# Layer 0 of a four-layer convolution network: the order of two kinds of expansion rows, and the place of some loads

## The chip, the cores and the metric

The kernel runs on one NeuronCore of one Trainium2 chip. The metric is the device time of one execution in microseconds, all four layers in one launch; lower is better. The time before is the median of three runs.

## The reference, cut to what matters

The input `x` is (4, 64, 256, 256) in float32. Four layers follow each other, each `x = x + layer(group_norm(x))`. Only layer 0 is touched by the change:

```python
x = einsum('bchw,oc->bohw', group_norm(x), w_in)      # 64 -> 384 channels: the "expansion"
# every 8x8 patch: rfft2, times a filter per channel, irfft2
x = conv_general_dilated(x, w_dw, padding=1, feature_group_count=C)   # 3x3, per channel
x1, x2 = split(x, 2, axis=1)
x = einsum('bchw,oc->bohw', gelu(x1) * x2, w_out)     # 192 -> 64 channels: the "projection"
```

The later layers are a 3x3 convolution, a thresholded choice between two 1x1 convolutions, and a product in Fourier space.

## The kernel before, in words

Layer 0 works on patches of 8x8 pixels. A batch item has 32 rows of patches. A **block** `p` covers 11 of them plus one row of halo, so there are three blocks for each item and 12 in all (`blocks`, `p` = 0 to 11); the rows of a block are `t` = 0 to 11. The first block of an item has no row `t = 0` and the last has no row `t = 11`, because the image ends there. The hidden channels are worked in four quarters (`kb` = 0 to 3). So there are 48 rounds `(p, kb)`, and each has two parts:

1. **Expansion** (`expand(p, kb, t)` for each row). TensorE multiplies normalized patches (the stationary operand, from `xn`) by the quarter's weights `win` into two PSUM buffers `psu`, one for each half of the image (`s` = 0, 1). ScalarE then copies half 0, and VectorE half 1, from PSUM into the big SBUF tile `u`. There are two kinds of rows. A **paired** row (`pairs` true) puts two patches into one stationary operand of 128 columns (line 444): 16 products in the program, 32 matmul and 32 weight-load instructions in the profile, and four copies on each engine (line 459). An **unpaired** row has one patch per stationary (line 450): 64 matmul and 64 weight-load instructions, and three copies on each engine (lines 461 to 463).
2. **Convolution** (`convolve(p, kb, g)` for 12 groups `g`). The patch filter and the 3x3 convolution are one product with a prepared matrix `w` (lines 494 and 503), then a gelu on ScalarE (line 510), a product on VectorE (line 511) and a store of `g` to DRAM by GpSimd's queue (line 514). Before the groups 0, 3, 6 and 9 stands one `unit()`: a piece of the projection of the block before (`project`, lines 591 and 598, TensorE; lines 607 to 618, VectorE), followed by `load_half`, which asks SyncE for the residual rows (`load_r`, line 559) and the stored `g` (`load_g`, lines 546 and 550) of a later unit.

PSUM is handed out by `banks()`: four buffers of two banks in turn. A row of the expansion takes two, so two rows are in flight; a convolution group takes two, a unit one.

The order on TensorE, VectorE, ScalarE and SyncE is the order of the program (`manual_schedule`). The engines meet by semaphores alone, so SyncE issues each DMA as soon as those before it in its own order are issued and its buffer is free, whatever row TensorE is at. SyncE's loads in a round are: `load_w` (the matrices `w` of a later pair of groups, line 471), `load_half` (in `kb` 0 also at rows 5 and 8), and `load_next`. The last is called four times in a round. For `kb` 0 to 2 it loads a piece of the next item for its group statistics (`load_stats`, line 627), which VectorE works at groups 1, 2, 4 and 5 (`next_stats`, line 320). For `kb` 3 it loads one of the first four new rows of the next block (`load_x`, line 418), which ScalarE normalizes at groups 1, 2, 3 and 4 (line 256).

Of the kernel before, what the change touches and what calls it, by code (L numbers as in the profile page):

```python
# [121 lines left out]
class _Net:  # L122
# [152 lines left out]
    def _layer0(self, ctx, dst):  # L275
# [5 lines left out]
        def banks(name):  # L281

            return pp.tile([128, 2, 512], F32, tag=f"p{next(turn) % 4}", name=name)
# [11 lines left out]
        NR = 11  # L295
# [118 lines left out]
        def load_x(row, p_x=p_x):  # L414
            b, i = row
            x0[row] = p_x.tile([128, P, HW2], F32, tag="x", name=f"x0_{b}_{i}")
            for s in range(2):
                nc.sync.dma_start(x0[row][halves[s]], a["x"][b, :, P * i : P * i + P, s * HW2 : (s + 1) * HW2])

        def normalize_x(row):  # L420
            b, i = row
            xn = xns[row] = p_xn.tile([128, HW2 // P, P, P], F32, tag="xn", name=f"xn_{b}_{i}")
            self.normalize(
                xn.rearrange("p m r w -> p r m w"), x0.pop(row).rearrange("p r (m w) -> p r m w", w=P), 0, b
            )
# [6 lines left out]
        def expand(p, kb, t):  # L432

            b, i0 = blocks[p]
            ps = [banks(f"psu_{p}_{kb}_{t}_{s}") for s in range(2)]
            xn = xns[b, i0 + t]
            lo, hi = halves
            pairs = t % 2 == 0
            for k in range(2):
                for m in range(4):  # L440
                    n, at = 2 * (4 * k + m), slice(2 * PB * m, 2 * PB * (m + 1))
                    for s in range(2):
                        if pairs:
                            nc.tensor.matmul(  # L444
                                ps[s][:, k, at], xn[halves[s], n : n + 2].rearrange("p n r w -> p (n r w)"),
                                win[halves[s], kb, 0 : 2 * PB], start=True, stop=True,
                            )
                            continue
                        for odd in range(2):
                            nc.tensor.matmul(  # L450
                                ps[s][halves[1 - odd], k, at], xn[halves[s], n + odd].rearrange("p r w -> p (r w)"),
                                win[halves[s], kb, PB * (1 - odd) : PB * (3 - odd)], start=True, stop=True,
                            )
            at = lambda h, o: u[h, :, t * CW + o : t * CW + o + 8].rearrange("p c (s m) -> p c s m", s=2)
            for s, copy in enumerate((nc.scalar.copy, nc.vector.tensor_copy)):
                v = ps[s][:, :, 0 : 8 * PB].rearrange("p s (m c) -> p c s m", m=4)
                if pairs:
                    for h, o, k, c in ((lo, O1, lo, 0), (hi, O2, lo, PB), (lo, E1 + 1, hi, 0), (hi, E2 + 1, hi, PB)):
                        copy(at(h, 8 * s + o), v[k, c : c + PB])  # L459
                    continue  # L460
                copy(at(slice(0, 128), 8 * s + 1), v[:, 0:PB])
                copy(at(hi, 8 * s + E2 + 1), v[lo, PB:])
                copy(at(lo, 8 * s + O1), v[hi, PB:])  # L463

        def load_w(j):

            p, k = divmod(j, HID // 8)
            if p >= NB:
                return
            w = wl[j] = p_w.tile([128, 2, 4, NC], F32, tag="w", name=f"w_{j}")  # L470
            nc.sync.dma_start(
                w, wts[k // 8][:, :, :, 4 * (k % 8) : 4 * (k % 8) + 4].rearrange("h i k c n -> (h i) k c n")
            )
# [89 lines left out]
        def load_half(p, r, half):  # L563
            if 0 <= p < NB and r < P:
                if half == 0:
                    load_r(p, r)
                load_g(p, r, half)
# [56 lines left out]
        def load_stats(b, j):  # L624
            t = st[b, j] = p_x.tile([128, 4, W], F32, tag="x", name=f"st{b}_{j}")
            for s in range(2):
                nc.sync.dma_start(t[halves[s]], src_t[b, :, j, s])

        def next_stats(b, j):
            if b not in bst0s:  # L630
                bst0s[b] = new_bst0(b)
            input_stats(st.pop((b, j)), j, bst0s[b])
            if j == NJ - 1:
                self.norms.append(self.group_norm_parts(0, b, bst0s.pop(b)))
# [6 lines left out]
        with ordered:  # L641
# [51 lines left out]
            for p in range(NB + 1):  # L693
                units = iter([(r, half) for r in range(P) for half in range(2)] if p > 0 else [])
                ahead, first = 1, []
                if p == NB:
                    ctx_u.close()
                    sources.append([pool("l0g1e", 6), pool("l0g6e", 6), pool("l0re", 3)])
                    ahead = 3
                for r in range(ahead):  # L700
                    for half in range(2):
                        first.append((p - 1, r, half))
                        if p == NB:
                            load_half(*first.pop())

                def unit():
                    at = next(units, None)
                    if at:
                        project(p - 1, *at)
                        load_half(p - 1, at[0] + ahead, at[1])  # L710

                if p == NB:
                    for k in range(2 * P):
                        unit()
                    while self.norms:
                        self.next_norms()
                    break
                b, i0 = blocks[p]
                rows = rows_of(p)
                after = rows_of(p + 1) if p + 1 < NB else []  # L720
                fresh = [row for row in after if row not in xns]
                for t in (0, NR):
                    if not 0 <= i0 + t < NP:
                        nc.gpsimd.memset(rows_u[:, :, t], 0.0)
                nk = [] if b + 1 >= B else list(range(p % NI * NJ // NI, (p % NI + 1) * NJ // NI))
                loaded, begun = [], iter(fresh[:4])

                def load_next(kb):
                    if kb == 3:
                        row = next(begun, None)  # L730
                        if row:
                            load_x(row)
                    elif nk:
                        loaded.append(nk.pop(0))
                        load_stats(b + 1, loaded[-1])

                for kb in range(4):
                    for t in range(NR + 1):
                        if 0 <= i0 + t < NP:
                            expand(p, kb, t)  # L740
                        if t in (5, 8) and first:
                            load_half(*first.pop(0))
                        if t == NR - 2:
                            load_w(p * (HID // 8) + NG * kb // 2 + 3)
                        if t >= NR - 1:
                            load_next(kb)
                    for g in range(NG):
                        G = NG * kb + g
                        if g % 2 == 0 and g > 0:
                            load_w(p * (HID // 8) + G // 2 + 3)  # L750
                        if g % 3 == 0:
                            unit()
                        convolve(p, kb, g)
                        if g < 2:
                            load_next(kb)
                        if g < NG - 1:
                            self.next_norms()
                        if kb < 3:
                            if g in (1, 2, 4, 5) and loaded:
                                next_stats(b + 1, loaded.pop(0))  # L760
                        elif 0 <= g - 1 < len(fresh):
                            k = g - 1
                            normalize_x(fresh[k])
                            if k + 4 < len(fresh):
                                load_x(fresh[k + 4])
                for row in rows:
                    if row not in after:
                        xns.pop(row)
# [728 lines left out]
```

## Time and profile before

| | us |
|---|---|
| median of 3 runs | 6502.17 |
| lowest, highest run | 6493.61, 6522.05 |
| the profiled execution | 6525.09 |
| its span, first to last instruction | 6523.3 |
| TensorE busy in the span | 6001.2 (92%) |
| VectorE busy | 4272.8 (66%) |
| ScalarE busy | 3240.4 (50%) |

The profiled execution lies 23 us above the median. In lines of the timeline the first number is the start in us from the span's start, the second the length in us, then follow engine, source line, operation, the tile written and the tiles read, and the number of instructions (x32); a bracket gives the idle time before and what ended it. PE is TensorE, PEld its weight loads, DVE is VectorE, ACT is ScalarE, POOL is GpSimd, SPq is SyncE's queue. Layer 0 fills the span up to about 3840 us.

### The profile page before, as it was taken

The numbers are of one execution on the slowest core, as the hardware profiler recorded it, in microseconds if no ns is written. First come the engines' busy times: TensorE is split into PE (matmuls) and PEld (weight loads), VectorE is DVE, ScalarE is ACT, GpSimd is POOL, SyncE is SP. The second block draws the span as 40 slices with busy tenths as digits, with TensorE's granted clock in tenths as the row PEclk, the third lists the DMA queues.
The fourth block names the chain that finished last, engine by engine and source line by source line (L and its number), as shares of the span: only waits on it lengthen the run. The fifth ranks groups of instructions, "written<-read, shape, count | busy, mean of one in ns | idle before, by whom it ended". The sixth has DMA issues, their size and how long they took to land.

```text
span 6523.3 us, 238228 instructions
## 1 busy us (share of the span) xinstructions
PE 6001.2 (92%) x106712; PEld 3199.7 (49%) x106712; DVE 4272.8 (66%) x5924; ACT 3240.4 (50%) x4564; POOL 1046.6 (16%) x1646
## 2 busy tenths in 40 slices
PE   2999999999999999999999977999899999999988
PEld 1455555555555555555555543333344444443566
DVE  5556665565655565655555546999798889885355
ACT  4344434344443444443444314777787778773211
POOL 3111111111111111111111111111122222221011
PEclk9999999999999999999999978999999999999855
DMA  8487879787888787886868779999576666667899
GB/s 242 136 218 214 230 207 232 218 242 219 245 220 243 219 236 206 229 223 199 228 195 226 207 198 244 226 229 228 148 180 174 170 173 181 170 176 268 325 353 398
DMA packets 878510, 1447.67 MB, mean 222 GB/s; under 512 B 77252, under 2 KB 586452, under 8 KB 875444
## 3 DMA queue, kind: packets, MB, share of 16 engines
q1 hardware_dynamic: 725284, 923.09, 55.9%
q0 software_dynamic: 148672, 500.14, 22.1%
q8 instruction: 843, 13.81, 0.9%
q10 hardware_dynamic: 3536, 9.20, 0.6%
q14 instruction: 175, 1.43, 0.1%
HBM read 932.08 MB, written 500.04 MB: 220 GB/s over the span
## 4 chain that ended last, share of the span: by engine, by line
PE 83%; DMA 7%; ACT 5%; issue 2%; DVE 2%; SPq 1%; POOL 0%; ACTq 0%; DVEq 0%; POOLq 0%
PE pc L503 18%; PE pc L494 12%; PE m L880 10%; PE psu L444 9%; PE one L1121 9%; PE div L1080 7%; ACT u L459 4%; PE psu L450 4%; PE po L591 4%; PE psz L1110 2%; DMA x<-x 2%; PE po L598 2%; DMA g<-g 2%; PE psa L1308 2%; DMA x<-in_x_dram 1%
## 5 line engine op out<-in xcount | busy, mean ns | idle before, releaser
L511 DVE TENSOR_TENSOR h<-h,pc 128x374 f32<-128x374 f32 x1152 | 575.3, 541 | 1216.7 <-ACT h L510 1216.5
L510 ACT ACTIVATE h<-pc 128x374 f32<-128x374 f32 x1152 | 493.1, 480 | 1762.0 <-PE pc L503 1745.9
L503 PE MATMUL pc<-u,w 64*16 64x374 f32 (+2 forms) x27648 | 1241.4, 480 | 3.0 <-issue 3.0
L514 POOL DMA_DIRECT2D g<-h x576 | 414.8, 720 | 2990.7 <-DVE h L511 2800.8
L494 PE MATMUL pc<-u,w 64*64 64x374 f32 x9216 | 881.2, 488 | 6.7 <-DVE u L463 3.9
L503 PEld LDWEIGHTS pc<-u,w 64*16 64x16 f32 (+2 forms) x27648 | 413.3, 92 | 763.5 <-issue 761.6
L444 PE MATMUL psu<-win,xn 64*128 64x96 f32 x8704 | 625.7, 283 | 137.2 <-ACT u L459 124.1
L459 DVE COPY u<-psu 64x384 f32<-64x384 f32 x1088 | 604.3, 555 | 155.1 <-PE psu L444 143.5
L444 PEld LDWEIGHTS psu<-win,xn 64*128 64x128 f32 x8704 | 574.8, 193 | 206.2 <-ACT u L459 159.9
L459 ACT COPY u<-psu 64x384 f32<-64x384 f32 x1088 | 560.5, 515 | 221.1 <-PE psu L444 201.0
L1066 DVE TENSOR_TENSOR q<-xn 128x2313 f32<-128x2313 f32 (+2 forms) x256 | 628.0, 2496 | 1.9 <-ACT xn L256 1.7
L1121 PE MATMUL one<-z,wp 32*32 32x512 f32 x16384 | 598.0, 599 | 19.0 <-issue 14.9
L256 ACT ACTIVATE xn<-x,nb,r 128x1024 f32<-128x1024 f32 (+3 forms) x272 | 486.7, 1792 | 212.4 <-DMA x<-x 140.5
L494 PEld LDWEIGHTS pc<-u,w 64*64 64x64 f32 x9216 | 332.2, 132 | 451.1 <-issue 359.7
L1067 ACT ACTIVATE q<-q 128x2313 f32<-128x2313 f32 (+2 forms) x256 | 529.0, 2087 | 30.8 <-DVE q L1066 29.3
L450 PE MATMUL psu<-win,xn 64*64 64x96 f32 x17408 | 456.5, 253 | 79.3 <-issue 48.6
L1080 PE MATMUL div<-q,ones 64*32 64x512 f32 x8192 | 471.1, 602 | 13.8 <-ACT q L1067 10.9
L1121 PEld LDWEIGHTS one<-z,wp 32*32 32x32 f32 x16384 | 367.2, 103 | 229.7 <-issue 88.3
L450 PEld LDWEIGHTS psu<-win,xn 64*64 64x64 f32 x17408 | 396.8, 138 | 121.4 <-issue 66.7
L1154 POOL DMA_DIRECT2D x<-r x512 | 273.9, 544 | 977.8 <-DVE r L1151 963.9
L591 PE MATMUL po<-g,wo 128*64 128x176 f32 (+1 forms) x3072 | 314.9, 348 | 74.3 <-DMA g<-g 37.9
L880 PE MATMUL m<-t,wk 64*64 64x512 f32 x3072 | 341.1, 588 | 0.0
(162 smaller groups left out, 6672.9 us busy)
## 6 DMA issues: line engine op xcount, KB each, us to landing
g<-h POOLq DMA_DIRECT2D x576, 374.0 KB, 6.4
x<-x SPq DMA_DIRECT2D x240, 640.0 KB, 6.4
w<-wt SPq DMA_DIRECT2D x288, 448.0 KB, 7.0
x<-x SPq DMA_DIRECT2D x100, 1024.0 KB, 14.2
g<-g SPq DMA_DIRECT2D x414, 187.0 KB, 5.0
g<-g SPq DMA_DIRECT2D x736, 93.5 KB, 5.3
x<-in_x_dram SPq DMA_DIRECT2D x256, 256.0 KB, 8.2
x<-o POOLq DMA_DIRECT2D x128, 512.0 KB, 8.2
```

Source lines behind the costliest of these rows:

```text
L444: nc.tensor.matmul(ps[s][:, k, at], xn[halves[s], n : n + 2].rearrange("p n r w -> p (n r w)"), win[halves[s], kb, 0 : 2 * PB], start=True ...
L450: nc.tensor.matmul(ps[s][halves[1 - odd], k, at], xn[halves[s], n + odd].rearrange("p r w -> p (r w)"), win[halves[s], kb, PB * (1 - odd) ...
L459: copy(at(h, 8 * s + o), v[k, c : c + PB])
L494: nc.tensor.matmul(out(C * c, C, k, h), w[halves[h], k, 2 * (G % 2) + c, 0:C], cells(h, 4 * g + 2 * k + c, 0, 0), start=True, stop=False, ...
L503: nc.tensor.matmul(out(q, m, k, h), w[halves[h], k, 2 * (G % 2) + c, c0 : c0 + m], cells(h, 4 * g + 2 * k + c, down, right), start=False, ...
L511: nc.vector.tensor_mul(h[:, k], h[:, k], ps[k][:, 1, 0:L])
L591: nc.tensor.matmul(out(k, s, x), wo1, moving(g1[:, 2 * k], 2 * half + k, s, x), start=(x == 0), stop=False, skip_group_check=True,)
L880: nc.tensor.matmul(rows2(m)[halves[j], s], w[dx][halves[s]], ts[n][halves[s], i, 2 * j : 2 * j + 2, dx : dx + W], start=(dx == 0), stop=(d ...
L1066: nc.vector.tensor_sub(d, p0, p1)
L1067: nc.scalar.activation(d, d, AF.Square)
L1080: ins = nc.tensor.matmul(ps[quarters[j], h], ones[halves[h]], q[n, g, k][halves[h], r + 2 * j : r + 2 * j + 2, o : o + W], start=(m == 0), ...
L1121: ins = nc.tensor.matmul(rows2(ps[g])[quarters[j], k], w[quarters[i]], z[quarters[i], h, 2 * j + dy : 2 * j + dy + 2, dx : dx + W], tile_p ...
```

## The change

In `expand`, a row is paired when `t` is below 6, where before it was paired when `t` is even. The numbers of paired and unpaired rows stay the same in every block: 6 and 6, or 5 and 6 in the first block of an item, 6 and 5 in the last. The rows 0 to 5 are now paired and the rows 6 to 11 unpaired.

In the loop over rounds, `load_w` moves from row 9 to row 11 (`NR` is 11), and the four `load_next` calls move from rows 10 and 11 and groups 0 and 1 to row 11 and groups 0, 1 and 2.

```diff
-            pairs = t % 2 == 0
+            pairs = t < (NR + 1) // 2
...
-                        if t == NR - 2:
+                        if t == NR:
                             load_w(p * (HID // 8) + NG * kb // 2 + 3)
-                        if t >= NR - 1:
                             load_next(kb)
                     for g in range(NG):
                         G = NG * kb + g
...
                         convolve(p, kb, g)
-                        if g < 2:
+                        if g < 3:
                             load_next(kb)
```

## The prediction

> **What bounds the kernel now.** I read the costliest groups by shape first, then the timeline of one expansion engine by engine, then the same expansion in time windows, then a stall.
>
> ```profile
> L444 PE MATMUL psu<-win,xn 64*128 64x96 f32 x8704 | 625.7, 283 | 137.2 <-ACT u L459 124.1 <-issue 7.1 <-DVE h L511 5.8
> L450 PE MATMUL psu<-win,xn 64*64 64x96 f32 x17408 | 456.5, 253 | 79.3 <-issue 48.6 <-ACT u L463 24.7 <-ACT xn L256 5.8
> L459 DVE COPY u<-psu 64x384 f32<-64x384 f32 x1088 | 604.3, 555 | 155.1 <-PE psu L444 143.5
> ```
>
> In the 48 expansions TensorE is idle for 137.2 + 79.3 = 216 us. Two causes matter: 124.1 us of waiting for the copies of line 459 (ended by "ACT u L459"), and 55.7 us (48.6 + 7.1) "issue". The convolution has nearly none, so the expansion is where the change can act.
>
> ```profile
> 1503.76 2.20 PE L444 MATMUL psu<-win,xn 64*128 64x96 f32 x32 [0.79 <-ACT u L459]
> 1505.89 1.55 PE L450 MATMUL psu<-win,xn 64*64 64x96 f32 x64
> 1508.06 2.34 PE L444 MATMUL psu<-win,xn 64*128 64x96 f32 x32 [0.62 <-ACT u L459]
> ...
> 1525.82 1.49 PE L591 MATMUL po<-g,wo 128*64 128x160 f32 x16 [0.62 <-ACT u L459]
> ...
> 1576.63 2.03 PE L444 MATMUL psu<-win,xn 64*128 64x96 f32 x32
> ...
> 1505.99 2.26 DVE L459 COPY u<-psu 64x384 f32<-64x384 f32 x4 [0.45 <-PE psu L444]
> 1508.29 0.56 DVE L461 COPY u<-psu 128x384 f32<-128x384 f32 x1
> 1508.86 0.55 DVE L462 COPY u<-psu 64x384 f32<-64x384 f32 x1
> 1509.43 0.56 DVE L463 COPY u<-psu 64x384 f32<-64x384 f32 x1
> 1510.44 2.26 DVE L459 COPY u<-psu 64x384 f32<-64x384 f32 x4 [0.45 <-PE psu L444]
> ```
>
> Two rows take 4.45 us (1505.99 to 1510.44). Neither engine fills that: VectorE copies 2.30 + 1.70 us and idles 0.45, TensorE works 2.03 + 1.55. The cause is that alternate rows give every paired row the same two of the four PSUM buffers. Matmuls (2.03) and VectorE's copies (2.26) of paired rows cannot overlap each other, and with about 0.15 of handing over that loop is 4.45. The unpaired rows' loop (1.55 + 1.70) has slack.
>
> ```profile
> 1503.00:1507.00 4.00, 3.24 (x84) 3.15 (x88) 3.47 (x7) 3.30 (x8) 0.00 (x0) 1.00 1.03 308
> 1507.00:1511.00 4.00, 3.32 (x73) 2.91 (x66) 3.45 (x7) 3.19 (x7) 0.00 (x0) 1.00 1.10 217
> 1515.00:1519.00 4.00, 3.39 (x95) 3.17 (x88) 3.77 (x7) 3.34 (x7) 0.00 (x0) 1.00 0.01 4
> 1361.00:1371.00 10.00, 7.33 (x177) 6.67 (x177) 8.66 (x16) 7.82 (x16) 0.00 (x0) 1.00 1.01 244
> ```
>
> The last three columns are TensorE's clock, DMA share and GB/s. An expansion of kb 1 to 3 (these rows: p 4, kb 2, first row at 1499.45) has full DMA engines for some 11 us, then almost none. In kb 0 (last row: p 4, first row at 1343.13) they are full to the end.
>
> ```profile
> 2204.80 0.54 PE L450 MATMUL psu<-win,xn 64*64 64x96 f32 x11
> 2208.72 2.51 PE L450 MATMUL psu<-win,xn 64*64 64x96 f32 x53 [3.38 <-issue]
> 2211.16 3.73 PE L444 MATMUL psu<-win,xn 64*128 64x96 f32 x32
> q8 instruction: 843, 13.81, 0.9%
> ```
>
> The "issue" idle time is instruction supply. Queue 8 moved 13.81 MB in 843 packets, 16.4 KB each, against 213,424 matmuls and weight loads and some 2,450 semaphore instructions of TensorE: 256 instructions a packet. In the records of the trace the stalls sit at one position in every 256, 1.2 to 1.7 us after the end of a packet, and that packet was asked for one block (256 instructions) earlier. So a block can't be entered sooner than the packet's start delay + 1.14 (median packet) + 1.42 after the block before it; I use delay + 2.55 us.
>
> **The change part by part: the rows.** Now neighbours of one kind use the two buffer pairs in turn, so matmuls of one row run beside copies of the one before. The loops halve: (2.03 + 2.26 + 0.15) / 2 = 2.22 us paired, (1.55 + 1.70 + 0.15) / 2 = 1.70 unpaired. VectorE's own work is longer, 2.30 and 1.73 with its gaps, and becomes the bound; ScalarE copies 2.13 and 1.54 and stays under it. From the first matmul: VectorE starts at 2.11 (1576.63 to 1578.74), works six paired rows to 15.9, and has finished row 9 at 22.8; TensorE then does row 11 in 1.6 and is at the projection at 24.4. Before, that took 26.37 (1499.45 to 1525.82): 1.95 saved. Where row 11 is missing: 22.7 against 24.19, 1.5 saved; where row 0 is missing: 22.1 against 23.56, 1.45. Sixteen expansions of each: 31 + 24 + 23 = **78 us**, of 216 idle. VectorE's last copy ends at 26.3, about when the projection's 2.1 us end, and only the later products of the first group read that row.
>
> **The change part by part: instruction supply.** 256 instructions last 5.9 us in alternation (192 in 4.45), 9.2 in paired rows, but only 3.45 in unpaired ones. The unpaired rows now run from about 14 to 24 us and enter some three blocks. Packet start delays before, medians over the blocks p 1 to 11, by time after the first row: kb 1 and 2: 3.8 us at 4 to 8 us, 1.3 at 12 to 16, 0.9 at 16 to 20, 0.8 at 20 to 24. kb 3: 4.1, 1.5, 2.3, 0. kb 0: 2.1, 2.1, 4.6, 3.6. With 2.55 added, the early ones exceed 5.9 now and won't exceed 9.2; the late ones come near 3.45 in kb 1 to 3 and exceed it twofold in kb 0. I worked each of these 44 expansions through row by row with its own recorded delays. Stalls before, kb 0 to 3: 1.5, 0.9, 0.5, 0.8 us each; after: 4.3, 0.8, 0.6, 1.4. Eleven of each: +31, -1, +1, +6, and some 2 for p 0: **39 us lost**, four fifths of it in kb 0. Bounds: no stalls after at all saves the 40 us of before (3.7 x 11); the late delays of kb 0 in every expansion would add 3.5 x 33 = 115.
>
> A stall also costs clock. Behind the 3.38 us stall above, a paired row takes 3.73 us for 2.03, and the window 2212 to 2216 has a granted clock of 0.50. The records show 15 such drops in layer 0 after p 0, mostly in kb 1 to 3 and after stalls from 1.5 us on; 3.4 to 10 us at half. I expect about as many, moved to kb 0: nothing, within 20 us either way.
>
> [...]
>
> **The change part by part: the loads.** SyncE runs ahead, so the row at which a call stands matters only through its order: at 1499.66, in the first row, it already issues the `load_w` that stands at row 9. `load_w` passes nothing but its own `load_next`: nothing. The second load now stands behind the `load_half` of group 0, whose `load_g` waits for that unit's matmuls; the third and fourth move by a group, the fourth behind `load_w` of group 2. So 512 KB leaves the busy start of the expansion (about 2 us of DMA at 230 to 300 GB/s), which helps supply in kb 0 a little. The second load then goes out where the third does now, at 1532.91, and needs about 7 us (the page: 8.2 for these loads); VectorE wants it at 1540.02. In the records loads from this place land 9 to 12 us after the first convolution matmul and are wanted at 12. If one is 2 us late, VectorE's statistics, and behind them the projection's additions, move; the product of group 3 has 0.39 us and its PSUM buffers about 2 us of cover. ScalarE's normalization in kb 3 is alike. I take 0; a whole microsecond in 38 expansions would be 38.
>
> **Sum.** -78 + 39 = -39 us. Against the profiled execution 6525.1 to 6486; it was 23 us above the median, so against the median 6502 to **6463**.
>
> **Rivals.** (1) Supply keeps up once DMA is idle: in kb 1 to 3 no stall is left. For it: windows with a DMA share of 0.01. Against: delays of 0.8 to 1.5 us are recorded there. -78 + 31 - 24 = -71, 6431; hidden in kb 0 too, -118, 6384. Chance 0.18. [...] (2) No measurable difference: kb 0 pays the clock on top (about two 3.4 us windows at half, some 2 us, in 11 expansions) or loads come late; -39 + 22 = -17, 6485. Against: the second load no longer burdens kb 0. Chance 0.26. (3) Slower: supply of the dense rows. If every late packet of kb 1 to 3 has kb 3's delay of 2.3 us, a block takes 4.85 for 3.45, and 2.5 blocks cost 3.5 us where I count 0.9: 2.6 x 33 = +86, so +47, 6549. It decides from 1.2 us more stall per expansion (39 / 33). For it: no block anywhere in layer 0 took under 4.08 us, so 3.45 is unproven. Against: quiet DMA at that time. Chance 0.13. That the change does nothing is no rival: the paired rows' loop is broken by construction.
>
> **How the numbers follow.** My forecast has 0.43 and its own range 6445 to 6480. Measurement here tells about 0.5% from nothing, 32.5 us, so faster means under 6469.7. The forecast gives 0.34 of that and rival 1 all of its 0.18, with 0.05 from milder forms of rival 2: 0.57. Slower is rival 3, 0.13. The rest, 0.30, is the same. The range 6405 to 6520 leaves out the hidden fetch in full and most of rival 3.
>
> **What would show it.** Right: in paired rows VectorE's copies back to back at 2.3 us; the wait of line 444 for "ACT u L459" down from 124 us to below 40; clean expansions of kb 1 and 2 at 24.4 us for 12 rows; stalls of line 450 under "issue" up from 48.6, mostly in kb 0. Wrong: two paired rows still apart by more than 2.4 us; issue waits of 3 us in unpaired rows of kb 1 and 2; statistics of line 320 waiting for loads at group 2.

## The result, and the profile after

The change takes 6486.01 us (median of 20 runs, 6469.98 to 6506.94) against 6509.86 us for the kernel before in the same session: a ratio of 0.9963, with a 95% interval of 0.9949 to 0.9978. On another chip, with 6 runs, it was 0.9949 (0.9933 to 0.9964). So it is faster by 24 to 33 us where 39 were forecast. By the bound of 0.5% named in the prediction its first measurement counts as "the same", which had a chance of 0.30; "faster" had 0.57. The time lies in the range of 6405 to 6520, but above the forecast's own 6445 to 6480. Times and ratios in this document leave out one slow execution, 10213.84 us at a granted clock of 0.727, of the kernel with kb 0 alternating and kb 3's loads as before.

The two profiled spans, 6523.3 and 6490.0 us, differ by 33.3 us. Layer 0, from its first expansion to its last convolution, holds 22.8 of that; the rest lies in stages that the change does not touch.

The groups by shape after, in the same view as before:

```profile
L444 PE MATMUL psu<-win,xn 64*128 64x96 f32 x8704 | 604.4, 285 | 63.2 <-ACT u L459 40.7 <-DVE h L511 10.9 <-ACT xn L256 7.6
L450 PE MATMUL psu<-win,xn 64*64 64x96 f32 x17408 | 494.0, 252 | 99.8 <-issue 65.7 <-ACT u L459 11.7 <-DVE u L463 8.5
L256 ACT ACTIVATE xn<-x,nb,r 128x1024 f32<-128x1024 f32 x128 | 158.9, 1241 | 149.1 <-DMA x<-in_x_dram 149.0
```

The wait of line 444 for ScalarE's copies fell from 124.1 to 40.7 us; the issue wait before line 450 rose from 48.6 to 65.7. Two things are new. Line 450 is busy 37 us longer than before (456.5), while line 444 is busy 21 us less (625.7 before); a single matmul of line 450 is no longer than before (252 ns, before 253), and the kernel with the rows alone changed shows the same 494 us. And ScalarE's normalization waits 149.0 us for x loads, where it was 68.0.

The timeline of a clean expansion after (p 4, kb 2; TensorE's rows, then VectorE's):

```profile
1481.68 3.81 PE L444 MATMUL psu<-win,xn 64*128 64x96 f32 x64
1485.97 9.10 PE L444 MATMUL psu<-win,xn 64*128 64x96 f32 x128 [0.48 <-ACT u L459]
...
1506.05 1.48 PE L591 MATMUL po<-g,wo 128*64 128x160 f32 x16
...
1483.78 13.75 DVE L459 COPY u<-psu 64x384 f32<-64x384 f32 x24 [0.47 <-PE psu L444]
```

VectorE makes the 24 copies of six paired rows without a pause: 13.75 / 6 = 2.29 us a row. The projection starts 24.37 us after the first row (1481.68 to 1506.05). And the same stretch of kb 0 after (p 4), timeline of TensorE and of one normalization of ScalarE's:

```profile
1319.44 2.20 PE L444 MATMUL psu<-win,xn 64*128 64x96 f32 x32
1322.77 3.39 PE L444 MATMUL psu<-win,xn 64*128 64x96 f32 x32 [1.13 <-DVE h L511]
...
1351.78 2.19 PE L450 MATMUL psu<-win,xn 64*64 64x96 f32 x47 [3.58 <-issue]
1353.90 1.86 PE L591 MATMUL po<-g,wo 128*64 128x160 f32 x16
...
1320.53 1.24 ACT L256 ACTIVATE xn<-x,nb,r 128x1024 f32<-128x1024 f32 x1 [4.34 <-DMA x<-in_x_dram]
```

and one window of it, with the busy time of each engine (TensorE's matmuls first) and at the end the granted clock (TensorE's, 1.00 is full speed), the DMA share and GB/s:

```profile
1325.00:1331.00 6.00, 5.36 (x49) 5.11 (x49) 2.93 (x6) 4.11 (x9) 0.00 (x0) 0.50 0.99 214
```

It lasts 34.5 us against 28.4 before. At its start ScalarE has waited 4.34 us for an x load, in a normalization of the round before, and what stands behind it is late. TensorE then waits 1.13 us for a buffer that VectorE's product of line 511 has to give free, and the window 1325 to 1331 has a granted clock of 0.50. At its end TensorE is idle for 3.58 us under "issue", at the entry of a block of 256 instructions.

By kind of round, from the first row to the projection, means over the blocks p 1 to 11: kb 0 27.2 us before, 31.8 after; kb 1 26.3 and 23.9; kb 2 25.7 and 23.5; kb 3 26.6 and 24.1. So kb 1 to 3 gained 78.5 us in all and kb 0 lost 50.5, with 6.3 more in its first projection piece. The convolution of kb 3 behind that piece got longer by 1.1 us (11 in all).

### The profile page after: what moved, and what is told of

Same layout as the page of the kernel before. It is cut to its first block, busy times and chain, and to the rows that moved or that the text cites. A ratio compares the mean times of both kernels' runs of the same rounds, so it can differ in the third digit from the quotient of the medians.

```text
span 6490.0 us, 238212 instructions
## 1 busy us (share of the span) xinstructions
PE 6025.7 (93%) x106712; PEld 3225.2 (50%) x106712; DVE 4272.2 (66%) x5924; ACT 3239.9 (50%) x4564; POOL 1047.5 (16%) x1646
## 3 DMA queue, kind: packets, MB, share of 16 engines
q1 hardware_dynamic: 725284, 923.09, 56.1%
## 4 chain that ended last, share of the span: by engine, by line
PE 76%; DMA 9%; DVE 7%; ACT 3%; issue 3%; SPq 1%; POOL 0%; DVEq 0%; ACTq 0%; POOLq 0%
PE pc L503 17%; PE pc L494 11%; PE m L879 10%; PE one L1120 9%; PE div L1079 7%; PE psu L444 5%; DVE u L459 5%; PE psu L450 4%; PE po L591 4%; DMA x<-in_x_dram 3%; PE psz L1109 2%; DMA x<-x 2%; DMA g<-g 2%; PE po L598 2%; PE psa L1307 2%
## 5 line engine op out<-in xcount | busy, mean ns | idle before, releaser
L444 PE MATMUL psu<-win,xn 64*128 64x96 f32 x8704 | 604.4, 285 | 63.2 <-ACT u L459 40.7
L256 ACT ACTIVATE xn<-x,nb,r 128x1024 f32<-128x1024 f32 (+3 forms) x272 | 486.8, 1793 | 293.5 <-DMA x<-in_x_dram 149.0
L450 PE MATMUL psu<-win,xn 64*64 64x96 f32 x17408 | 494.0, 252 | 99.8 <-issue 65.7
L450 PEld LDWEIGHTS psu<-win,xn 64*64 64x64 f32 x17408 | 428.4, 136 | 159.4 <-issue 89.9
```

The costliest lines, as they stand in the source:

```text
L444: nc.tensor.matmul(ps[s][:, k, at], xn[halves[s], n : n + 2].rearrange("p n r w -> p (n r w)"), win[halves[s], kb, 0 : 2 * PB], start=True ...
L450: nc.tensor.matmul(ps[s][halves[1 - odd], k, at], xn[halves[s], n + odd].rearrange("p r w -> p (r w)"), win[halves[s], kb, PB * (1 - odd) ...
```

## The experiments

Theory A: what the rows gain is partly given back by the moved x loads of kb 3, which land late and hold ScalarE, in kb 3 and into the next kb 0. Theory B: kb 0 loses because dense rows (the unpaired ones, 128 instructions in some 1.7 us) run there while DMA is full (a share of 1.13 from 1344.54 to 1348.91 us of the kb 0 above) and TensorE's instructions come late. The rivals are named in each expectation. "Rows-only" is the first kernel below.

**Rows grouped, loads as before.** The first hunk of the change alone.

> Rows 0 to 5 paired, 6 to 11 unpaired as in the change; every load where it was before. Theory A (the moved loads cost time: the four loads of kb 3 arrive late, ScalarE waits for them in the normalizations of kb 3 and into the first rows of the next kb 0): without the move the convolution of kb 3 goes back from 50.4 to 49.3 us and kb 0's expansion from 31.8 to about 28.5; kb 1 to 3 keep their 2.3 us each. About 55 to 65 us under before, 30 to 40 under the change. Theory B (the 4.6 us that kb 0's expansion grew by are instruction supply in the dense rows alone): kb 0 stays at 31 us or more, and the result lies within 12 us of the change, about 25 under before. Theory C (the second load in the busy start of the expansion matters, so its removal was what helped kb 1 to 3): slower than the change by 10 us or more.

Measured: 6451.16 us, ratio 0.9935 (0.9915 to 0.9955), 0.3% under the change's first measurement. The convolution of kb 3 is back at 49.4 us (50.4 in the change), kb 0's expansion at 29.4 (31.8 with the moved loads), kb 1 to 3 keep their gain (73 us). Its line 450 and its normalization, in the groups by shape:

```profile
L450 PE MATMUL psu<-win,xn 64*64 64x96 f32 x17408 | 493.8, 251 | 98.4 <-issue 62.2 <-ACT u L459 11.6 <-DVE u L463 9.2
L256 ACT ACTIVATE xn<-x,nb,r 128x1024 f32<-128x1024 f32 x128 | 158.9, 1241 | 41.0 <-DMA x<-in_x_dram 40.7
```

A fits, though the size falls short: 42 us under before by the ratio, where A had 55 to 65. C falls. B has its part: 29.4 is still 2.2 over before.

**Loads moved, rows alternating.** The other hunks alone.

> Rows alternate as before; only the loads are moved as in the change. Theory A: the late x loads cost by themselves, 20 to 35 us slower than before, with the waits of the normalization (line 256) for x loads up from 68 us to about 140. Theory B: within 10 us of before, waits of line 256 not above 80 us. My prediction took 0 for this part, with 38 us as its bound.

Measured: 6498.94 us, ratio 0.9999 (0.9984 to 1.0013): no difference. The waits of line 256 for x loads, 144.3 us, are as A has them, but the time is not. Its line 450:

```profile
L450 PE MATMUL psu<-win,xn 64*64 64x96 f32 x17408 | 450.2, 251 | 64.6 <-issue 28.1 <-ACT u L463 21.6 <-DVE h L511 8.2
```

Line 450's issue wait fell from 48.6 to 28.1 us. That fits one load less at the start of the expansion, with instructions that come earlier: kb 1 to 3 gain 31 us in the profile, and kb 0 and kb 3's convolution lose about 18. Both theories missed this gain. With grouped rows little of it is left (78.5 us with moved loads, 73 without), which fits the few instructions that paired rows need at that time (64 in 2.29 us).

**Unpaired rows first.** `pairs = t >= (NR + 1) // 2`, loads as before.

> The order turned round: rows 0 to 5 unpaired, 6 to 11 paired, loads as before (in the first block of an item 5 unpaired and 6 paired rows, one more paired than before). VectorE has nearly the same work and the PSUM buffers are used in the same balanced way. If VectorE's copies alone set the time of an expansion, this is as fast as the rows-only kernel within 15 us. If instruction supply matters as the prediction says, the dense rows now fall into the time of full DMA engines: blocks of 256 instructions that take 3.45 us of work wait for packets that start 3 to 4 us late, 2.5 to 3 us each for two blocks in every expansion of kb 1 to 3, so about 5 us x 33 = 165 us slower than the rows-only kernel, some 100 us slower than before, with the issue idle time before line 450 well over 150 us.

Measured: 6596.03 us, ratio 1.0146 (1.0126 to 1.0165): 94 us slower than before, as instruction supply has it (100). Part of this is the clock: in the rounds of the blocks p 1 to 11 it stood at half for 201 us, in rows-only for 72. Its group of line 450:

```profile
L450 PE MATMUL psu<-win,xn 64*64 64x96 f32 x17408 | 517.6, 270 | 218.6 <-issue 171.2 <-ACT u L463 33.1 <-ACT xn L256 4.8
```

and TensorE's timeline of one of its expansions:

```profile
1533.44 6.11 PE L450 MATMUL psu<-win,xn 64*64 64x96 f32 x228
...
1547.48 1.55 PE L450 MATMUL psu<-win,xn 64*64 64x96 f32 x30 [2.97 <-issue]
1548.96 8.20 PE L444 MATMUL psu<-win,xn 64*128 64x96 f32 x96
```

In all, the rows and copies are those of rows-only: the first block of an item has one paired row more and the last has one less. Their order is worth 145 us.

**kb 0 alternating, kb 1 to 3 grouped, loads as before.** `pairs = t < (NR + 1) // 2 if kb else t % 2 == 0`.

> Rows of one kind together in kb 1 to 3, alternating in kb 0; every load where it was before. kb 1 to 3 gain 2.3 us each, kb 0 is as before: 33 x 2.3 + p 0's 5 = about 80 us under before (6430). It lies under the rows-only kernel by what grouping costs in kb 0: 15 us by theory A, 45 us by theory B. If it is above the rows-only kernel, grouping pays in kb 0 too.

Measured: 6421.05 us, ratio 0.9880 (0.9860 to 0.9899): by the ratio 78 us under before, 30 under rows-only, between A's and B's figures. Grouping costs time in kb 0 and gains in the others. This beats both kernels.

```profile
L450 PE MATMUL psu<-win,xn 64*64 64x96 f32 x17408 | 480.1, 249 | 83.5 <-ACT u L463 31.8 <-issue 26.7 <-ACT u L459 7.8
```

**kb 0 all paired.** `pairs = t < (NR + 1) // 2 or kb == 0`, loads as before.

> In kb 0 every row is paired, in kb 1 to 3 the rows are grouped; every load as before. In kb 0 VectorE copies 12 x 2.30 = 27.6 us, TensorE is at the projection some 25.5 to 27.5 us after the first row, and a block of 256 instructions lasts 9.2 us, longer than any packet's delay plus 2.55, so kb 0 should hold no issue wait. Theory B (kb 0's extra time when grouped is instruction supply in dense rows while DMA is full): kb 0's expansion at about 27 us in the mean, against 29.4 grouped and 27.1 alternating, so 6415 to 6430, with issue idle time before line 450 near that of the kernel with kb 0 alternating or below it. Rival: something else in kb 0 (late x loads, the clock) holds it, then its expansion stays at 29 us or more and the time is at 6445 or above.

Measured: 6436.86 us, ratio 0.9884 (0.9864 to 0.9905), on a chip where before took 6510.09. The time is over B's range and under the rival's. kb 0's expansion takes 26.7 us and has no issue wait left in the blocks p 1 to 11, where rows-only has 44.4 us in all. What remains of line 450's is in the other rounds:

```profile
L450 PE MATMUL psu<-win,xn 64*64 64x96 f32 x13056 | 362.4, 247 | 42.1 <-issue 18.2 <-ACT u L459 7.4 <-ACT u L463 5.5
```

Without dense rows kb 0 is faster than grouped (29.4), although VectorE copies more. B holds.

**The change with kb 3's loads as before**, and **rows grouped with only kb 3's loads moved.** In the first, rows 9 to 11 and groups 0 and 1 as before `if kb == 3`; the second the other way round.

> The change, but in kb 3 the loads (load_w and the four x loads) stand where they were before; in kb 0 to 2 they are moved. Theory A (the gap of 27 us between rows-only and the change comes from the x loads of kb 3, whose late landing holds ScalarE in the normalizations and in the first rows of the next kb 0): the whole gap comes back, 6445 to 6460, waits of line 256 for x loads back from 149 to about 40 to 70 us, convolution of kb 3 at 49.4 us. Rival A2 (the gap is from the moved statistics loads of kb 0 to 2): it stays at the change's 6475 to 6490.

> The other half of the kernel with kb 3's loads back: rows grouped as in the change, loads moved in kb 3 alone, as before in kb 0 to 2. Theory A (the late x loads of kb 3 are what the moved loads cost): the time of the change itself, 6480 to 6492 where before is 6505, and 15 to 35 us above rows-only; waits of line 256 for x loads at 140 us or more. Rival: the loads of kb 0 to 2 share the cost; then it lies at the rows-only level, 6445 to 6460.

> The change as it is, on the same chip as the others of this call: 0.996 of before by its first measurement; within 8 us of the kernel with only kb 3's loads moved by theory A.

Measured: 0.9920 (0.9896 to 0.9944; 6465.06 us on a chip where before took 6510.09) with kb 3's loads back, and 0.9965 (0.9949 to 0.9982; 6473.03 us) with them alone moved. The change again had 0.9949 (6465.14 us) on the chip of the latter, 7.9 us from it. The normalizations with kb 3's loads back and with them alone moved:

```profile
L256 ACT ACTIVATE xn<-x,nb,r 128x1024 f32<-128x1024 f32 x128 | 158.9, 1241 | 74.1 <-DMA x<-in_x_dram 74.1
L256 ACT ACTIVATE xn<-x,nb,r 128x1024 f32<-128x1024 f32 x128 | 158.9, 1241 | 157.5 <-DMA x<-in_x_dram 157.3
```

Kernels with late x loads and grouped rows stand at 0.9963, 0.9949 and 0.9965, those without at 0.9935 and 0.9920: some 0.3%, 20 us, though the intervals of single pairs touch. The rival, the statistics loads of kb 0 to 2, falls.

**The change with kb 0 alternating**, and **the same with kb 3's loads as before.**

> The change with kb 0 alternating. Theory A and B together: it loses only what the late x loads cost (ScalarE's waits, 11 us in kb 3's convolution and 10 to 15 in kb 0), so 15 to 25 us above the kernel with kb 0 alternating and loads as before (6421), 6436 to 6446. If the two parts of the change do not act on each other, it is above it by 35 to 40 us as the change is above its own rows-only kernel; if the loads cost nothing without dense rows in kb 0, it is equal to 6421 within 8 us.

> Alternating rows in kb 0, grouped in kb 1 to 3; loads moved in kb 0 to 2, as before in kb 3. If the moved statistics loads relieve instruction supply in the busy start of the expansions (kb 0 alternates still, kb 1 and 2 have paired rows there and need it little): 0 to 10 us under the kernel with kb 0 alternating and all loads as before (6421). If they only add load to the convolution: 0 to 10 us above.

Measured: 0.9887 (0.9867 to 0.9908; 6440.96 us) and 0.9869 (0.9848 to 0.9890; 6424.36 us). Against 0.9880 these are +5 and -7 us, within the intervals. So late x loads cost little beside alternating rows in kb 0, less than the 15 to 25 us expected, and the moved statistics loads can't be told from no change here. Why late x loads cost more beside grouped rows in kb 0 stays open.

**Every row paired.** `pairs = True`, loads as before.

> Every row paired in every kb, all loads as before: no dense rows anywhere. If VectorE's copies bound a grouped expansion at 2.30 us a paired row, TensorE reaches the projection at 2.1 + 10 x 2.3 + 2.1 = 27.2 us in 12 rows and 24.9 in 11, so 25.7 in the mean in kb 1 to 3 with hardly a stall, against 23.9 grouped: 33 x 1.8 = 60 us slower than the kernel with only kb 0 all paired (0.988 of before), so 0.996 to 0.999 of before, and issue idle time of line 444 under 15 us. If supply stalls cost the grouped rows more than their shorter copies gain, it is level with that kernel or faster (0.988 or less).

Measured: 6501.26 us, ratio 1.0002 (0.9991 to 1.0013), slightly over the range given. Nearly all expansions of kb 1 to 3 in the blocks p 1 to 11 take 27.10 or 24.81 us (27.2 and 24.9 expected). Its group of line 444:

```profile
L444 PE MATMUL psu<-win,xn 64*128 64x96 f32 x17408 | 1199.0, 280 | 78.3 <-ACT u L459 49.7 <-ACT xn L256 5.6 <-DVE h L511 2.5
```

"issue" is no longer among the three largest causes. VectorE's copies are the bound of a grouped expansion, and the dense rows are worth having where instructions come in time (0.9884 with all rows paired in kb 0 alone, 1.0002 in every kb).

## Why the prediction was right or wrong

**The rows: right.** The prediction had the projection at 24.4, 22.7 and 22.1 us after the first row; the clean expansions, those without a stall, took 24.37, 22.65 and 22.08. The wait of line 444 for the copies fell to 40.7 us, where the sign was "below 40". The PSUM loop was the cause.

**Instruction supply: right in kb 0, wrong in kb 1 to 3.** The forecast was 31 us more in kb 0 and 6 more in kb 1 to 3. In the expansions of the blocks p 1 to 11, TensorE's idle time that ended in "issue" went from 13.3 to 48.1 us in kb 0, which is 35 more, but from 38.2 to 14.4 in kb 1 to 3, which is 24 less. After the change kb 1 to 3 stand 0.75, 0.35 and 0.9 us over their clean times (0.8, 0.6 and 1.4 forecast). So the stalls after were sized nearly right; those before were taken too small, at 2.2 us for the three rounds of a block where the trace has 3.5. The 118 us of rival 1, in which the 40 us of before go too, needed kb 0 without stalls, and it had 48.1 us of them.

**The clock: a term put at 0 that was not.** "About as many, moved to kb 0" was the forecast. In the records of the blocks p 1 to 11 the half clock held for 17 us in kb 0 and 58 in kb 1 to 3 before; after, for 102 us in kb 0 and none elsewhere. If half of that time is lost, which is an estimate, kb 1 to 3 got back 29 us and kb 0 paid 43, so +14 net, inside the 20 us allowed. With it kb 0 nearly adds up: rows 19 us less, issue waits 35 more, clock 43 more, 59 in all, for 57 measured. In kb 1 to 3 the rows give some 55 of the 78.5 us (33 expansions, 24.8 to 23.1 clean). The other 23 are fewer issue waits and a better clock; the two overlap, and no run parts them.

**The total: partly luck.** For the blocks p 1 to 11 the forecast comes to about 50 us less in kb 1 to 3 and 12 more in kb 0. Measured were 78.5 less and 57 more, with 11 more in kb 3's convolution. Two errors of opposite sign kept the time inside the range.

**The loads: "I take 0" held beside alternating rows, not beside grouped ones.** This is the step that failed. With alternating rows the moved loads came to nothing in sum (0.9999), with grouped rows they cost some 20 us. The statistics are as forecast: line 320 waits 13.7 us for its loads, 18.2 before. But "ScalarE's normalization in kb 3 is alike" overlooked the chain behind it. Each further x load waits on SyncE for the normalization four rows earlier, and the fourth of the moved loads now stands behind one of these and behind `load_w` of group 2. The fourth normalization in kb 3 of p 4, in ScalarE's timeline of before:

```profile
1626.46 1.24 ACT L256 ACTIVATE xn<-x,nb,r 128x1024 f32<-128x1024 f32 x1
```

and of after, where it waits 3.95 us for its load:

```profile
1607.69 1.24 ACT L256 ACTIVATE xn<-x,nb,r 128x1024 f32<-128x1024 f32 x1 [3.95 <-DMA x<-in_x_dram]
```

The lateness is passed on from load to load, and the last normalization delays ScalarE's work for kb 0's first rows. In the expansions of kb 0 in the blocks p 1 to 11, TensorE's waits for VectorE's product of line 511 come to 10.9 to 19.0 us in the five profiles with late x loads (10.9 in the change), and to 1.8 to 6.2 in the eight without. The half clock in kb 0 held for 102 us in the change, 82 in its second profile, and 65 in rows-only. The 11 us in kb 3's convolution do not follow from these loads alone: with only kb 3's loads moved line 256 waited 157.3 us, and that convolution took 49.4 us, as in rows-only. So the cost stayed within the bound of 38 us, and the runs show it at the start of kb 0; how it comes to 20 us beside grouped rows and to almost nothing beside alternating ones stays open.

**The rivals.** Rival 2 was the nearest: its time (6485) came about, and so did both its mechanisms, the clock in kb 0 and late loads. It had two windows of 3.4 us at half clock in each kb 0; the change has 9.3 us. Rival 1 was half there: supply in kb 1 to 3 left little stall, 14.4 us in 33 expansions. Rival 3 did not happen, but the kernel with unpaired rows first shows that its mechanism is real (171.2 us of issue wait before line 450).

## What to carry to other kernels

When a buffer rotation and an alternation of work have the same period, the heavy kind always meets the same buffers; break the period before looking for a faster instruction (here a clean expansion of 12 rows went from 26.37 to 24.37 us). Place instruction-dense stretches where DMA is quiet (here 6451.16 us, against 6596.03 with the order turned round), and measure that by stretch, not by the page's mean. Before moving a load "by one step", follow the loads that wait for its consumer: here ScalarE's waits for x loads went from 68.0 to 149.0 us. That cost some 20 us beside grouped rows in kb 0 and nothing that could be measured beside alternating ones.

## What the runs showed of the hardware

The page has the instruction packets on the same 16 DMA engines as the data: queue 8, of kind instruction, with 0.9% of their span, queue 1 with 56.1%. In the change's trace, where the DMA share was 0.02, a block of 256 instructions was entered 3.4 us after the one before it at the best. In kb 0 the packets behind its stalls of over 2 us started 3 to 6 us after the block before was entered, with DMA shares of 1.00 to 1.16 in that time, and a block took up to 8.6 us. The order of the rows decided how much of this TensorE waited for: line 450 had 171.2 us of issue wait before it with the unpaired rows first, 62.2 with the paired rows first.

The clock fell to half after some short pauses and not after others. TensorE's timeline before the change, in p 6, kb 1, and at a second place:

```profile
2058.01 2.19 PE L450 MATMUL psu<-win,xn 64*64 64x96 f32 x45 [1.83 <-issue]
...
1966.70 2.48 PE L444 MATMUL psu<-win,xn 64*128 64x96 f32 x32 [2.55 <-DVE h L511]
```

and windows around them, with the granted clock third from the end:

```profile
2056.00:2060.00 4.00, 2.17 (x52) 1.89 (x45) 1.81 (x4) 1.53 (x3) 0.00 (x0) 0.74 0.02 4
2060.00:2064.00 4.00, 4.00 (x101) 3.78 (x96) 2.84 (x6) 2.67 (x6) 0.00 (x0) 0.83 0.01 2
...
1964.00:1968.00 4.00, 1.45 (x24) 1.14 (x18) 1.89 (x4) 3.04 (x4) 0.60 (x1) 1.00 1.05 320
```

Behind the pause of 1.83 us the two windows have granted clocks of 0.74 and 0.83, which is one stretch of 3.4 us at half. Behind the longer pause of 2.55 us the clock stayed at 1.00, in that window and the next. So the length of the pause alone does not decide; what else does, the runs do not show.
